# Forward transform: the stationary operand of two of eight pieces of x, 128 columns wide instead of twice 64

## The chip, the cores and the metric

One core of a Trainium2 chip runs the whole kernel in one launch. The metric is the device time of an execution in microseconds (us). TensorE is PE in the profile (its loads of stationary operands are PEld), VectorE is DVE, ScalarE is ACT, GpSimd is POOL, SyncE is SP.

## The reference, cut to what matters

Two layers follow each other on x of 16 images, 64 channels, 128 x 128 pixels, all in fp32. The change is in the first step of the first layer, the two-dimensional Hartley transform, of which only 20 x 20 modes are used:

```python
def dht_2d(x):
    return (fftn(x, axes=(2, 3)).real - fftn(flip(x, axis=(2, 3)), axes=(2, 3)).imag)
...
x_ht = dht_2d(x)                                               # 16 x 64 x 128 x 128
out_ht[:, :, :20, :20] = compl_mul2d(x_ht[:, :, :20, :20], w1) # mixes channels per mode
y = gaussian_smoothing_4d(dht_2d(out_ht) / (H * W)) * mask
# second layer: group norm, AFNO on 32 x 32 modes, group norm, 1x1 features,
# two shared experts and 4 of 16 experts per image with GELU, residual
```

The transform is separable: a sum over the rows of an image with cosines and sines, then a sum over its columns. The kernel does both sums as matrix products, and folds the first layer's inverse, its smoothing and the second layer's group norm and spectrum into tables over modes.

## The kernel before, in words

The kernel has stages that follow each other. The forward transform takes x from DRAM and leaves 400 modes of each image and channel in x2. Then the modes are mixed (L294 to L365), then the spectrum goes through AFNO's two layers (from L420 on), and last, over most of the time, come the inverse transform, the features and the experts, image by image, in an order written out in PIECES (L965).

The forward transform loops over the 16 images (L263) and, in each, over eight pieces of eight channels (c0, L266). For a piece:

- SP loads xt, 128 rows x 8 channels x 128 columns, 512 KB (L268). Pool f_x has 10 such buffers, so that SP runs up to ten pieces ahead and then waits until PE has done with the oldest.
- PE multiplies each channel with fwd1, 128 x 64, of which 40 columns are cosines and sines of 20 frequencies (L273). The image is the stationary operand: 128 rows are summed over, and its columns become partitions of the result in PSUM, ps (pool f_p1, 4 buffers). The 128 columns go as two operands of 64: one matmul in each half of the array and of the partitions, written as `h` in L271 and L272.
- ACT copies ps to t1, turned so that the channels lie next to each other (L276).

When t1 has all 64 channels, `along_columns` (L225) is the second sum for that image: 40 matmuls (L233) with t1 as stationary operand, 128 x 64, and fwd2 as moving operand, into ps2. It is a generator: the loop runs it in portions behind pieces 1 to 5 of the next image (L279), so that the last image's portions come after the loop (L285). After its matmuls ACT copies half of ps2 (L238), DVE adds and subtracts to xm (L242 to L245) and adds xm, with the weights of the smoothing along the batch, to up to nine images of x2 (L254). When an image of x2 is complete, ACT writes its second half (L259, L260). ACT has one order: these two wait for DVE, and the copies of the next pieces (L276) stand behind them.

fwd2 is loaded on SP's queue after the first image's pieces (L281), the weights wk after all of x (L284). The loads of wn (L294) use memory that is free only when DVE has ended the transform.

The order on each engine in this stage is the program's, as the scheduler of the tile framework lets it stand.

Of the kernel before, what the change touches and what calls it, by code (L numbers as in the profile page):

```python
# [18 lines left out]
NB, C, N = 16, 64, 128  # L19
# [11 lines left out]
EC = 65  # L31
TILES = (0, 1, 2, 3, 6, 7, 4, 5)
EDGED = {0: (0, 16), 1: (64, 16), 4: (128, 16), 5: (192, 16), 2: (256, 1)}
BY_ACT = (0, 2, 4, 6)
CL = C // 2
NSL = 8
# [21 lines left out]
def constant_tables():  # L58
# [29 lines left out]
    for j in range(2):  # L88
# [3 lines left out]
        for r in (0, 64):  # L92
            inv2[r:r + 32, j], inv2[r + 32:r + 64, j] = np.cos(a32)[:, ns], -np.sin(a32)[:, ns]
    e_cols = np.concatenate([s_[8 * t:8 * t + 8] for t, (_, m) in EDGED.items() if m > 1 for s_ in sides] + [[32]])
    d1 = e1 - g1 * e
# [85 lines left out]
def hartley_afno_moe_kernel(ctx: ExitStack, tc: tile.TileContext, a: dict, out: bass.AP):  # L181
# [6 lines left out]
    def load(pool, name, shape, eng=None):  # L188
        t = pool.tile(shape, F32, name=name + "_sb", tag=name)
        src = a[name]  # L190
        if len(shape) == 3 and len(src.shape) == 2:
            src = src.rearrange("p (a b) -> p a b", b=shape[2])
        (eng or nc.sync).dma_start(t, src)
        return t
# [15 lines left out]
    with tc.tile_pool(name="modes", bufs=1) as mp:  # L210
# [6 lines left out]
        with tc.tile_pool(name="f_x", bufs=10) as xp, tc.tile_pool(name="f_t", bufs=2) as tp, \  # L217
                tc.tile_pool(name="f_c", bufs=1) as fc, \
                tc.tile_pool(name="f_p1", bufs=4, space=PSUM) as pp1, \
                tc.tile_pool(name="f_p2", bufs=2, space=PSUM) as pp2:  # L220
            fwd1 = load(fc, "fwd1", [P, W1], nc.gpsimd)
            fwd2 = None
            seen = set()

            def along_columns(b, t1):  # L225


                ps = pp2.tile([P, K // 2, W1], F32, name="ps2")
                for m in range(K // 2):
                    for t in range(2):  # L230
                        for h in range(2):
                            j = 2 * (2 * m + h) + t
                            nc.tensor.matmul(ps[h * C:(h + 1) * C, m, :], lhsT=t1[:, j, :],  # L233
                                             rhs=fwd2[:, j, :], start=(t == 0), stop=(t == 1))
                    if m in (1, 3, 5, 7):
                        yield
                pn = tp.tile([P, K // 2, K], F32, name="pn")
                nc.scalar.copy(pn, ps[:, :, K:2 * K])  # L238
                xm = tp.tile([P, K, K], F32, name="xm")
                for half, op in ((0, ALU.add), (1, ALU.subtract)):  # L240
                    to = xm[half * C:(half + 1) * C]
                    nc.vector.tensor_tensor(to[:, 0:1], ps[0:C, 0:1, 0:K], pn[0:C, 0:1], op)  # L242
                    nc.vector.tensor_tensor(to[:, 2:K:2], ps[0:C, 1:, 0:K],
                                            pn[0:C, K // 2 - 1:0:-1], op)
                    nc.vector.tensor_tensor(to[:, 1:K:2], ps[C:P, :, 0:K],  # L245
                                            pn[C:P, ::-1], op)
                xf = xm.rearrange("p a b -> p (a b)")
                for bo in range(NB):
                    g = float(gb[bo, b])
                    if g == 0.0:  # L250
                        continue
                    to = x2[:, 0, bo, :]
                    if bo in seen:
                        nc.vector.scalar_tensor_tensor(to, xf, g, to, ALU.mult, ALU.add)  # L254
                    else:
                        nc.vector.tensor_scalar(to, xf, g, None, ALU.mult)
                        seen.add(bo)
                    if not gb[bo, b + 1:].any():
                        nc.scalar.mul(x2[0:C, 1, bo], x2[C:P, 0, bo], -1.0)  # L259
                        nc.scalar.copy(x2[C:P, 1, bo], x2[0:C, 0, bo])  # L260

            behind = None
            for b in range(NB):  # L263

                t1 = tp.tile([P, 2 * K, C], F32, name="t1")
                for c0 in range(0, C, 8):  # L266
                    xt = xp.tile([P, 8, N], F32, name="xt")
                    nc.sync.dma_start(xt, a["x"][b, :, c0:c0 + 8])  # L268
                    ps = pp1.tile([P, 8, W1], F32, name="ps1")
                    for i in range(8):  # L270
                        for h in range(2):  # L271
                            cols = slice(h * 64, (h + 1) * 64)  # L272
                            nc.tensor.matmul(ps[cols, i, :], lhsT=xt[:, i, cols],  # L273
                                             rhs=fwd1, start=True, stop=True)
                    src = ps[:, :, 0:2 * K].rearrange("p c j -> p j c")
                    nc.scalar.copy(t1[:, :, c0:c0 + 8], src)  # L276

                    if c0 and behind:
                        next(behind, None)  # L279
                behind = along_columns(b, t1)  # L280
                fwd2 = fwd2 or load(fc, "fwd2", [P, 2 * K, W1])  # L281

            for k in range(K // 2 + 1):
                nc.sync.dma_start(wk[0:C, k], a["w"][k])  # L284
            for _ in behind:  # L285
                pass

        with tc.tile_pool(name="m_o", bufs=1) as op, tc.tile_pool(name="m_w", bufs=4) as wp, \
# [24 lines left out]
            for h in range(2):  # L313
                hs_ = slice(h * CL, (h + 1) * CL)
                for ri in range(2):
                    own_rows = slice(h * C + ri * CL, h * C + (ri + 1) * CL)
                    for ro in range(2):
                        c0 = (ri ^ ro) * P + h * CL
# [99 lines left out]
    with tc.tile_pool(name="s_o", bufs=1) as so, \  # L418
# [86 lines left out]
        for r in range(4):  # L505
            g = slice(r * CL, (r + 1) * CL)
            c0 = (r & 1) * C + (r >> 1) * CL
# [121 lines left out]
        for b in range(NB):  # L629
            xk = sw.tile([P, MD * MD], F32, name="xk")  # L630
            xr = sw.tile([P, MD * MD], F32, name="xr")
            for n in range(2):
                cols = slice(n * 512, (n + 1) * 512)
# [31 lines left out]
    with s3:  # L665
# [59 lines left out]
        def pixels(box, t):  # L725
# [13 lines left out]
            def evacuate():  # L739
# [3 lines left out]
                pv = ps.rearrange("p s (j i) -> p i (s j)", i=C)  # L743
                e0, nm = EDGED.get(t, (0, 0))
                at = 4 if nm > 1 and t not in BY_ACT else 0
                if t in BY_ACT:
                    nc.scalar.copy(hv, pv)
# [311 lines left out]
```

## Time and profile before

| | us |
|---|---|
| median of 3 runs | 1706.57 (1701.43 to 1714.94) |
| profiled execution, its own time | 1737.26 |
| its span, first to last instruction | 1735.3 |
| L273, first to last start | 6.3 to 239.0 |
| PE, DVE, ACT busy in the span | 1561.7, 1268.7, 1272.2 |
| PE busy from 90 to 140 us | 38.46 of 50 |
| last load of x issued | 211.8 |

A row of a group reads: line, engine, operation, output<-inputs, stationary operand (rows*columns), moving operand (rows x columns), count, then busy time in us, mean duration in ns, and the idle time of the engine just before, with what ended it. An fp32 matmul of the program stands there as two loads (LDWEIGHTS) and two matmuls (MATMUL). Matmuls are pipelined: one is shown as longer than the time until the next starts, so starts are compared here. "issue" is idle time that ended with nothing the profile shows. A row of stretches has its length, then busy time and count of PE, PEld, DVE, ACT and POOL, the granted clock of PE as a share, the busy share of the DMA engines, and GB/s. Queue rows give packets, MB and the share of 16 DMA engines.

### The profile page before, as it was taken

To read this page: it belongs to the slowest core of one execution; us is meant where nothing else is said; L and a number is where in the kernel's file an instruction comes from. 1 tells how busy PE (TensorE), PEld (TensorE's weight loads), DVE (VectorE), ACT (ScalarE), POOL (GpSimd) and SP (SyncE) were. 2 spreads that over 40 slices of the span, in tenths; PEclk is the share of its full clock that TensorE was granted. 3 is DMA by queue.
4 is the path that set the end of the run, shared out by engine and by line. 5 is a ranking of instruction groups with operands and counts; after the bars stand their busy time and mean duration, and the time that the engine had idled before them with its cause. 6 is when DMAs were issued, how large, how long until landed. Compare 5 with 4: busy or idle time off the path is not lost.

```text
span 1735.3 us, 62072 instructions
## 1 busy us (share of the span) xinstructions
PE 1561.7 (90%) x27656; PEld 856.4 (49%) x27656; DVE 1268.7 (73%) x1700; ACT 1272.2 (73%) x1631; POOL 148.9 (9%) x152
## 2 busy tenths in 40 slices
PE   6778758799997999999999999999999999999974
PEld 6778755233325554454454455545555455544421
DVE  0344423365763698988989889898898988989886
ACT  2233334255664898988989889898898988989875
POOL 0000002000130101101010010100101001010020
PEclk9999979899996999999999999999999999999997
DMA  9888864353574224555545555455554554545447
GB/s 382 296 304 303 313 132 120 81 123 94 126 180 101 42 44 79 92 87 88 74 80 87 92 89 75 77 86 94 87 73 78 90 93 87 73 80 79 66 66 114
DMA packets 398864, 205.07 MB, mean 118 GB/s; under 512 B 366842, under 2 KB 371942, under 8 KB 396222
## 3 DMA queue, kind: packets, MB, share of 16 engines
q1 hardware_dynamic: 394134, 193.76, 52.7%
q0 software_dynamic: 4464, 7.35, 1.7%
q8 instruction: 217, 3.56, 0.8%
q14 instruction: 49, 0.40, 0.1%
HBM read 109.86 MB, written 91.20 MB: 116 GB/s over the span
## 4 chain that ended last, share of the span: by engine, by line
PE 79%; issue 7%; DMA 4%; DVE 4%; ACT 3%; SPq 1%; POOL 0%; DVEq 0%; POOLq 0%; ACTq 0%
PE pe L897 37%; PE pe L736 9%; PE pe L716 7%; PE pe L807 6%; PE psx L639 6%; PE ps L273 6%; PE ps L233 3%; DMA spec_sb<-in_spec_dram 1%; PE psd L561 1%; ACT g L902 1%; PE psd L540 1%; DVE h L906 1%; PE pso L587 1%; PE pso L575 1%; DMA fwd_sb<-in_fwd_dram 1%
## 5 line engine op out<-in xcount | busy, mean ns | idle before, releaser
L902 ACT ACTIVATE g<-pe,wl 128x1024 f32<-128x1024 f32 x512 | 553.7, 1210 | 12.3 <-PE pe L897 12.2
L897 PE MATMUL pe<-f,wl 64*64 64x512 f32 x4096 | 501.3, 607 | 5.5 <-DMA wl<-exd,ati 5.5
L906 DVE SCALAR_TENSOR_TENSOR h<-g,wt,h 128x1024 f32<-128x1024 f32 x384 | 472.2, 1279 | 32.9 <-ACT g L902 32.0
L902 ACT ACTIVATE g<-pe,vec_sb 128x1024 f32<-128x1024 f32 x256 | 269.0, 1114 | 80.3 <-PE pe L897 80.2
L906 DVE SCALAR_TENSOR_TENSOR h<-g,h 128x1024 f32<-128x1024 f32 x256 | 301.9, 1216 | 18.2 <-ACT g L902 18.2
L897 PEld LDWEIGHTS pe<-f,wl 64*64 64x64 f32 x4096 | 164.8, 136 | 220.1 <-issue 118.5
L897 PE MATMUL pe<-f,shw 64*64 64x512 f32 x2048 | 257.2, 618 | 1.3 <-DVE sco L849 0.4
L736 PEld LDWEIGHTS pe<-inv_sb,u 64*64 64x64 f32 x8192 | 170.8, 141 | 111.2 <-issue 85.8
L736 PE MATMUL pe<-inv_sb,u 64*64 64x64 f32 x8192 | 181.7, 226 | 36.6 <-issue 35.3
L273 PE MATMUL ps<-fwd_sb,xt 128*64 128x64 f32 x4096 | 155.5, 232 | 41.3 <-issue 35.0
L273 PEld LDWEIGHTS ps<-fwd_sb,xt 128*64 128x64 f32 x4096 | 144.7, 146 | 47.7 <-issue 41.4
L276 ACT COPY t<-ps 128x320 f32<-128x320 f32 x128 | 53.9, 426 | 150.9 <-PE ps L273 150.4
L912 DVE SCALAR_TENSOR_TENSOR stg<-g,wt,h 128x1024 f32<-128x1024 f32 x128 | 158.3, 1278 | 0.0
L811 ACT ACTIVATE f<-pe,fba 128x1024 f32<-128x1024 f32 x128 | 154.6, 1219 | 3.0 <-PE pe L807 2.9
L716 PEld LDWEIGHTS pe<-inv_sb,bm 116*64 116x64 f32 x4096 | 129.1, 142 | 52.7 <-ACT g L902 34.9
L716 PE MATMUL pe<-inv_sb,bm 116*64 116x64 f32 x4096 | 138.0, 228 | 2.1 <-issue 1.3
L807 PE MATMUL pe<-h,fsa 64*64 64x512 f32 x1024 | 133.4, 594 | 1.4 <-DVE h L751 1.4
L639 PE MATMUL psx<-spec_sb,ot 100*32 100x512 f32 x1024 | 118.7, 606 | 10.5 <-DMA spec_sb<-in_spec_dram 10.5
L242 DVE TENSOR_TENSOR xm<-ps,pn 64x20 f32<-64x20 f32 x32 | 5.5, 171 | 162.9 <-ACT pn L238 162.7
L897 PEld LDWEIGHTS pe<-f,shw 64*64 64x64 f32 x2048 | 73.8, 136 | 101.4 <-issue 71.1
L870 POOL TENSOR_TENSOR dv<-root_e,dv 128x4 f32<-128x4 f32 x16 | 34.6, 2164 | 1020.3 <-DVE ati L873 907.5
L749 DVE COPY h<-pe 128x960 f32<-128x960 f32 x64 | 75.9, 1185 | 58.9 <-PE pe L736 58.9
(186 smaller groups left out, 1244.8 us busy)
## 6 DMA issues: line engine op xcount, KB each, us to landing
xt<-in_x_dram SPq DMA_DIRECT2D x128, 512.0 KB
out_dram<-stg SPq DMA_DIRECT2D x217, 256.0 KB
bmd<-bs SPq DMA_DIRECT2D x32, 512.0 KB
bm<-bmd SPq DMA_DIRECT2D x64, 256.0 KB
out_dram<-stg SPq DMA_DIRECT2D x31, 192.0 KB
wk<-in_w_dram SPq DMA_DIRECT2D x11, 320.0 KB
wn<-in_w_dram SPq DMA_DIRECT2D x11, 320.0 KB
spec_sb<-in_spec_dram SPq DMA_DIRECT2D x1, 3200.0 KB
```

The costliest lines, as they stand in the source:

```text
L273: nc.tensor.matmul(ps[cols, i, :], lhsT=xt[:, i, cols], rhs=fwd1, start=True, stop=True)
L276: nc.scalar.copy(t1[:, :, c0:c0 + 8], src)
L639: nc.tensor.matmul(ps[p0:p0 + CL], lhsT=ot[:, kc, b * C + h * CL:b * C + (h + 1) * CL], rhs=spec[:, kc, ri * 1024 + n * 512:ri * 1024 + (n ...
L716: nc.tensor.matmul(ps[s * C:(s + 1) * C, i // 8, i % 8], lhsT=bm[0:KR, 16 * q + i], rhs=inv1[0:KR, s], start=True, stop=True)
L736: nc.tensor.matmul(ps[half * C:(half + 1) * C, s, j * C:(j + 1) * C], lhsT=u[rs, t * 8 + j], rhs=inv2[rs, half], start=True, stop=True)
L749: nc.vector.tensor_copy(hv[:, at:], pv[:, at:])
L807: nc.tensor.matmul(ps[p * C:(p + 1) * C, half], lhsT=fsa[rows_, box["b"]], rhs=box["h"][t][rows_, p], start=True, stop=True)
L811: nc.scalar.activation(f, ps, AF.Gelu, bias=fba[:, box["b"]:box["b"] + 1], accum_out=box["sums"][:, t:t + 1])
L897: nc.tensor.matmul(ps[half * C:(half + 1) * C, p], lhsT=w[rows_], rhs=f[rows_, half], start=True, stop=True)
L902: newest[0] = nc.scalar.activation(g, ps, AF.Gelu, bias=bias)
L906: nc.vector.scalar_tensor_tensor(h, g, share(), h, ALU.mult, ALU.add)
L912: nc.vector.scalar_tensor_tensor(box["out"][-1][:, :, c0:c0 + 16], gv, share(), hv, ALU.mult, ALU.add)
```

## The change

In pieces 2 and 6 of each image (c0 of 16 and 48) each channel is one matmul with all 128 columns as stationary operand and one result over all 128 partitions. The other six pieces stay as they are. The loads of x, the tables, the buffers and the copies are the same.

```diff
+AS_WHOLE = (2, 6)
+WHOLE, SIDES = (slice(0, N),), (slice(0, N // 2), slice(N // 2, N))
...
                     for i in range(8):
-                        for h in range(2):
-                            cols = slice(h * 64, (h + 1) * 64)
+                        for cols in (WHOLE if c0 // 8 in AS_WHOLE else SIDES):
                             nc.tensor.matmul(ps[cols, i, :], lhsT=xt[:, i, cols],
                                              rhs=fwd1, start=True, stop=True)
```

## The prediction

> **What bounds the kernel now.** I read the page first. Over the span TensorE (PE) looks like the bound, and the instruction queue moves next to nothing:
>
> ```profile
> PE 1561.7 (90%) x27656; PEld 856.4 (49%) x27656; DVE 1268.7 (73%) x1700; ACT 1272.2 (73%) x1631; POOL 148.9 (9%) x152
> ...
> q8 instruction: 217, 3.56, 0.8%
> ...
> L273 PE MATMUL ps<-fwd_sb,xt 128*64 128x64 f32 x4096 | 155.5, 232 | 41.3 <-issue 35.0
> ```
>
> The changed line, L273, runs only from 6.3 to 239.0 us, so what counts is what bounds that stretch. In the waits of PE, from 5 to 242 us, and in those of SP's queue, the reader is to see who is late:
>
> ```profile
> PE ps L273 <- issue: 35.0, 21, 3.6
> PE ps L233 <- issue: 11.5, 9, 2.2
> PE ps L233 <- ACT t L276: 9.4, 7, 1.9
> ```
>
> ```profile
> SPq L268 <- PE ps L273: 138.9, 109, 4.3
> ```
>
> PE never waits for a tile of x; SP waits 109 times for PE to give an xt buffer back. So x is early and PE sets the pace. But PE itself stands still 30 times, 46.5 us, for "issue": nothing that the view can name. The timeline, matmul rows only, shows the pattern (start, duration, count, and in brackets the idle time before it):
>
> ```profile
> 99.80 0.27 PE L233 MATMUL ps<-fwd_sb,t 128*64 128x64 f32 x2 [1.60 <-issue]
> ...
> 104.99 2.02 PE L273 MATMUL ps<-fwd_sb,xt 128*64 128x64 f32 x62 [1.23 <-issue]
> ...
> 110.21 0.97 PE L273 MATMUL ps<-fwd_sb,xt 128*64 128x64 f32 x26 [0.95 <-issue]
> ...
> 110.97 0.69 PE L233 MATMUL ps<-fwd_sb,t 128*64 128x64 f32 x16
> ...
> 111.44 1.15 PE L273 MATMUL ps<-fwd_sb,xt 128*64 128x64 f32 x32
> ...
> 112.37 0.57 PE L233 MATMUL ps<-fwd_sb,t 128*64 128x64 f32 x12
> ...
> 112.72 1.15 PE L273 MATMUL ps<-fwd_sb,xt 128*64 128x64 f32 x32
> ...
> 113.65 0.51 PE L233 MATMUL ps<-fwd_sb,t 128*64 128x64 f32 x9
> ...
> 114.83 0.33 PE L233 MATMUL ps<-fwd_sb,t 128*64 128x64 f32 x3 [0.67 <-issue]
> ...
> 120.50 0.74 PE L273 MATMUL ps<-fwd_sb,xt 128*64 128x64 f32 x18 [1.70 <-issue]
> ```
>
> From the stall at 110.21 to that at 114.83 there are 26+16+32+12+32+9 = 127 matmuls, each with one load: about 256 instructions. Queue 8 moved 217 packets and PE ran 55,312 instructions: 255 per packet, and 3.56 MB over 217 is 16.4 KB. So I read "issue" as PE waiting for its next 256 instructions. Ends of stalls lie 5.19, 5.22, 4.62 and 5.67 us apart, 5.2 us a block, while 128 matmuls at 29 ns (32 in the 0.93 us from 101.23 to 102.16) need 3.7 us. A block comes back later than it is used up.
>
> [...] Two such loads in a row stand at L824:
>
> ```profile
> 571.32 0.64 PE L716 MATMUL pe<-inv_sb,bm 116*64 116x64 f32 x16
> ...
> 571.88 0.30 PEld L824 LDWEIGHTS pe<-gs,g1w_sb 128*128 128x128 f32 x2
> ...
> 301.61 3.60 PE L452 MATMUL psx<-ot,dev_sb 100*100 100x512 f32 x8
> ```
>
> One load lasts 188 ns and both 0.30 us, so they follow at 0.11 us[...]. [...] L716's last matmul lasts 0.22 us and ends at 571.96, so it began at 571.74, and L824 begins 0.14 us later where pairs follow at 0.058.
>
> **The change part by part.**
>
> 1. Instructions. Each fp32 matmul stands as two matmuls and two loads in the trace (4096 of L273 for 16x8x8x2 calls). A piece has 32 matmuls; whole, 16. With 32 pieces changed, 512 matmuls and 512 loads go: 1024 instructions, exactly 4 blocks of 256, so later blocks keep their borders. L273 and L233 together go from 42 blocks to 38. At 5.2 us a block this alone, if the fetch still sets the pace, is -21 us.
>
> 2. PE's own time. Two 64-column matmuls in the two halves of the array start together, a pair each 58 ns: a piece takes 16 x 58 = 0.93 us. Whole, a load of 128 columns every 108 ns; the matmul beside it is shorter (L452 gives (3.60-0.59)/7 = 0.43 us for 512 columns, so 54 ns for 64) and I let it lie beside the next load, as it does now. That is 16 x 0.108 = 1.73 us, plus about 0.09 for the drain going in and 0.12 coming out (L824 to L897 shows the same 0.07 us before the modelled end; 64 columns make the last matmul 0.05 longer than L824's). So 1.94 us, 1.0 more than now, 32 times: +32 us. PE's work in the stage goes from 42 x 3.7 = 156 to 188 us, or from 3.7 to 4.95 us a block. Not shown is a load of 128 columns beside matmuls of 64. Its ends are 0.93 us (no dearer than the pair) and 16 x (108+54) + 0.2 = 2.8 us (load and matmul one after the other). I take 1.94.
>
> 3. Stalls. Blocks take 1.24 us more, so a stall for instructions shrinks by as much. The chain of waits lists the stalls; those over 1.24 are 2.31, 2.24, 2.44, 1.56, 1.61, 1.53, 1.86, 1.60, 1.70, 1.67, 2.21, 2.08, 1.75, 1.66, 1.69, 2.58 and 3.58, and what is over sums to 13 us, 12 for 38 blocks. So 46.5 falls to 12: -34 us. This is the cover of part 2; without it, its 32 us would be paid.
>
> 4. ACT's wait. L233's first group of an image waits 7 times, 9.4 us, for t's last columns, because ACT stands behind DVE at L260 before it copies. Piece 6 runs in that time, and hides up to 0.9 us of each wait: between 0 and -6.6, I take -5. What is late next there is the same copy.
>
> 5. x and the fetch share the DMA engines. A block now covers 3.05 pieces (84 instructions each), then 3.37 (76): from 1.60 MB in 5.2 us, about 305 GB/s, to some 325. When x was loading at full rate, blocks came slower:
>
> ```profile
> 8.00:40.00 32.00, 23.82 (x701) 23.13 (x698) 3.06 (x11) 8.31 (x20) 0.00 (x0) 0.95 1.02 410
> ...
> 90.00:140.00 50.00, 38.46 (x1234) 37.23 (x1229) 23.11 (x59) 17.78 (x41) 0.00 (x0) 1.00 0.90 313
> ```
>
> There the stalls end 6.3 us apart (22.18, 28.44, 34.84, 41.03). A straight line from 5.2 at 313 to 6.3 at 410 adds 0.2 us at 20 GB/s more; I take half, on the 20 or so blocks that still stall: +2.5, ends 0 and +8.
>
> 6. Clock. Stalls of over 2 us are followed by spells at half clock (PEclk 0.93 from 140 to 190, 0.77 from 212 to 242). Fewer long stalls, fewer spells: -3, ends -6[...].
>
> SP's order, ACT's copies, PSUM buffers and DVE are untouched; the same ps1 tile is written. What follows (wn's loads wait for DVE at 248.4, then spec's) moves as a whole with the end of the stage.
>
> Sum: +32 - 34 - 5 + 2.5 - 3 = -7.5 us. The profiled execution, 1737.26 us for a span of 1735.3, would come to about 1730. It lies 1.8% above the median of the runs, 1706.57; I take the same -7 off that: 1699.5.
>
> **The rivals.** *The fetch stays the only bound* (0.28): blocks come back at 5.2 us whatever PE does, the 32 us all fit in stalls, ACT waits and half-clock spells: -21 us, about 1686. For it: three of four blocks stall now. Against it: 4.95 us a block is close to 5.2, and returns scatter (4.6 to 6.3), so the quick ones are wasted. *PE becomes the bound* (0.20), the slower side: in whole pieces the load does not lie beside the matmul, 2.8 us a piece. PE's work rises by 60, stalls fall by some 41, ACT's wait by 7, half-clock spells add 6: +18 us, about 1725. It decides where a whole piece takes more than some 2.2 us, where the sum changes sign. For it: no row shows such loads and matmuls in a row at full width. Against it: L452's loads of 100 columns lie wholly beside its matmuls. *Nothing is gained* (0.10): x, let go faster, holds the fetches up by as much as is saved (part 5 at its upper end): within 3 us of before.
>
> **How the numbers follow.** My forecast, most of the gain traded for PE time, has 0.42: -16 to +2 us by its own terms, 1691 to 1709. About 1%, 17 us, is what a measurement of this kernel can tell from no change. Faster by over 1%: most of the first rival and a tail of the forecast, 0.36; slower: most of the second, 0.19; within: 0.45. The range takes in -26 (all of part 1, 4 and 6) to +18: 1680 to 1725.
>
> **What would show it.** In the changed profile: L273 with 3584 matmuls, 512 of them 128 wide, starting 108 ns apart; q8 with 213 packets; "issue" before L273 and L233 down from 46.5 to 10 to 20 us; L233's wait for ACT about halved; the last L273 some 7 us before 239. A spacing of 160 ns shows the second rival, stalls as long as now the last one. Wrong altogether would be stalls no longer 256 instructions apart.

## The result, and the profile after

Over 18 runs of each the changed kernel took 1695.02 us (median; 1689.81 to 1705.51), the kernel before 1703.84 (1696.10 to 1717.33). The ratio is 0.9954, 95% interval 0.9935 to 0.9973: some 8 us faster (4.6 to 11 by the interval), where 7 were forecast. The profiled execution of the changed kernel took 1696.35 us by itself.

The page of the changed kernel has the counts that the change promises:

```profile
span 1693.5 us, 61048 instructions
...
PE 1559.1 (92%) x27144; PEld 846.6 (50%) x27144; DVE 1268.4 (75%) x1700; ACT 1273.8 (75%) x1631; POOL 153.3 (9%) x152
...
q8 instruction: 213, 3.49, 0.8%
```

That is 512 matmuls, 512 loads and four packets of instructions fewer: 1024 instructions for four packets, 256 each. (Lines from 33 on have moved by one or two: L273 is L274, L233 is L235, L276 is L277, L268 is L270, L254 is L256.) The groups of PE up to 245 us, kept apart by shape, say which matmuls are whole and what stood idle before them:

```profile
L274 PE MATMUL ps<-fwd_sb,xt 128*64 128x64 f32 x3072 | 112.0, 226 | 13.6 <-issue 7.6 <-DMA fwd_sb<-in_fwd_dram 5.9
...
L274 PE MATMUL ps<-fwd_sb,xt 128*128 128x64 f32 x512 | 64.8, 279 | 1.2 <-issue 1.2
```

PE's waits in the stage, in the columns total us, times, longest:

```profile
PE ps L274 <- issue: 8.8, 9, 4.0
...
PE ps L235 <- issue: 4.4, 5, 2.2
PE ps L235 <- ACT t L277: 3.6, 9, 0.5
```

Against 35.0 + 11.5 us of "issue" and 9.4 us of ACT before, 13.2 and 3.6 are left. Two stretches of the middle of the stage, with the columns as in the prediction:

```profile
90.00:140.00 50.00, 47.26 (x1152) 45.52 (x1151) 21.11 (x56) 17.63 (x42) 0.00 (x0) 1.00 0.91 318
140.00:190.00 50.00, 47.25 (x1144) 45.48 (x1144) 21.13 (x57) 16.61 (x41) 0.00 (x0) 1.00 0.93 321
```

PE counts as busy for 47 of 50 us where it was 38.5 in the first of these stretches: it is close to the bound now. The chain of waits shows a whole piece, the portion of L235 behind it and a split piece in a row, and later the step that follows the stage:

```profile
128.76 1.93 PE ps L274 x16
130.69 0.73 PE ps L235 x20
131.43 0.93 PE ps L274 x32
...
235.56 4.08 DMA wn<-in_w_dram
```

The timeline of the changed kernel has the 16 loads of that whole piece within 1.86 us (128.69 to 130.55), one of them 0.19 us long, so they follow at 0.11 us; from the start of its last matmul to that of L235's next (130.42 to 130.62) 0.20 us pass. The prediction and two expectations call such pauses at a change of shape drains; what PE does in them is not shown.

wn's first load on that chain started at 248.42 before, so the stage ends 12.9 us earlier between these two single executions; the medians differ by 8.8. Their spans differ by 41.8 us, and that is not the change: from DVE's last addition of the stage (248.4 before, 235.5 after) to the end it is 1487 us in the one and 1458 in the other. The same stretch took 1452 to 1462 us in all four experiments on one chip, 1479 to 1481 in the four on a second and 1483 to 1491 in the four on a third, whatever was done to the stage. It seems to go with the chip (the chip of the first two is not on record). So below, ratios come from runs beside the kernel before on the same chip, and traces are compared only within the stage.

### The profile page after: what moved, and what is told of

Its sections match the earlier page's. It is cut to its first block, busy times and chain, and to the rows that moved or that the text cites. A ratio compares the mean times of both kernels' runs of the same rounds, so it can differ in the third digit from the quotient of the medians.

```text
span 1693.5 us, 61048 instructions
## 1 busy us (share of the span) xinstructions
PE 1559.1 (92%) x27144; PEld 846.6 (50%) x27144; DVE 1268.4 (75%) x1700; ACT 1273.8 (75%) x1631; POOL 153.3 (9%) x152
## 4 chain that ended last, share of the span: by engine, by line
PE 70%; DMA 9%; issue 9%; ACT 5%; DVE 4%; SPq 1%; POOL 1%; DVEq 0%; POOLq 0%; ACTq 0%
PE pe L898 31%; PE pe L717 7%; PE ps L274 7%; PE psx L640 6%; PE pe L737 6%; PE pe L808 5%; DMA wl<-exd,ati 5%; ACT g L903 3%; PE ps L235 3%; DMA spec_sb<-in_spec_dram 1%; PE psd L562 1%; PE psd L541 1%; DVE h L907 1%; PE pso L588 1%; DMA edge_sb<-in_edge_dram 1%
## 5 line engine op out<-in xcount | busy, mean ns | idle before, releaser
L898 PE MATMUL pe<-f,wl 64*64 64x512 f32 x4096 | 496.3, 606 | 40.5 <-DMA wl<-exd,ati 39.3
L898 PEld LDWEIGHTS pe<-f,wl 64*64 64x64 f32 x4096 | 148.2, 135 | 267.2 <-issue 153.5
L903 ACT ACTIVATE g<-pe,vec_sb 128x1024 f32<-128x1024 f32 x256 | 269.2, 1115 | 10.9 <-PE pe L898 10.8
L898 PE MATMUL pe<-f,shw 64*64 64x512 f32 x2048 | 244.2, 595 | 0.8 <-DVE sco L850 0.4
L274 PE MATMUL ps<-fwd_sb,xt 128*64 128x64 f32 (+1 forms) x3584 | 175.4, 234 | 14.8 <-issue 8.8
L737 PEld LDWEIGHTS pe<-inv_sb,u 64*64 64x64 f32 x8192 | 154.6, 141 | 67.5 <-issue 41.3
L274 PEld LDWEIGHTS ps<-fwd_sb,xt 128*64 128x64 f32 (+1 forms) x3584 | 162.8, 148 | 19.4 <-issue 10.0
L277 ACT COPY t<-ps 128x320 f32<-128x320 f32 x128 | 53.8, 427 | 151.3 <-PE ps L274 150.9
L737 PE MATMUL pe<-inv_sb,u 64*64 64x64 f32 x8192 | 157.6, 226 | 2.4 <-issue 1.3
```

Source lines behind the costliest of these rows:

```text
L274: nc.tensor.matmul(ps[cols, i, :], lhsT=xt[:, i, cols], rhs=fwd1, start=True, stop=True)
L737: nc.tensor.matmul(ps[half * C:(half + 1) * C, s, j * C:(j + 1) * C], lhsT=u[rs, t * 8 + j], rhs=inv2[rs, half], start=True, stop=True)
L898: nc.tensor.matmul(ps[half * C:(half + 1) * C, p], lhsT=w[rows_], rhs=f[rows_, half], start=True, stop=True)
L903: newest[0] = nc.scalar.activation(g, ps, AF.Gelu, bias=bias)
```

## The experiments

All twelve, with the changed kernel first; "chip" is the median of the kernel before beside it. "Issue" and "ACT" are PE's waits in the stage (us, one profiled execution each). "Half" is the length of the spells at half clock (granted clock 0.50) that begin between 8 and 215 us, by the trace's clock record; where it is empty, no sum was made. "End" is DVE's last addition. Ratios with their intervals are formed over all runs, so they can differ a little from the quotient of two medians.

Two things limit what these columns say. The profiled executions of only_6, only_2, six_seven, x_on_15 and one_five took 6.6 to 12.9 us more than the median of their kernel, so their stalls and spells are not the usual size. And the clock record begins only with the first change to full clock: at 8.9 to 15.2 us in the kernels with an entry under "half", but at 28.8 us in three_whole and at 38.5 us in all_whole. Ahead of that PE went at half pace, as the first image's pieces of these two show (208 and 128 matmuls):

```profile
6.14 20.22 PE L274 MATMUL ps<-fwd_sb,xt 128*64 128x64 f32 x208 [6.14 <-DMA fwd_sb<-in_fwd_dram]
```

```profile
6.20 27.57 PE L274 MATMUL ps<-fwd_sb,xt 128*128 128x64 f32 x128 [6.20 <-DMA fwd_sb<-in_fwd_dram]
```

The first row is five split and three whole pieces (its shape is that of the first matmul). At 0.93 and 1.93 us they would take 10.4 us; the eight whole pieces of the second would take 15.4. Neither the column "half" nor a run's mean clock counts this time.

| kernel | chip | median | ratio (95%) | issue | ACT | half | end |
|---|---|---|---|---|---|---|---|
| before, profiled | | 1706.57 | | 46.5 | 9.4 | 13.7 | 248.4 |
| after (2, 6) | 1703.84 | 1695.02 | 0.9954 (0.9935-0.9973) | 13.2 | 3.6 | 3.4 | 235.5 |
| x_once_split | 1704.65 | 1641.30 | 0.9623 (0.9587-0.9659) | 7.1 | 0.5 | | 183.7 |
| x_once_whole | 1704.65 | 1674.52 | 0.9815 (0.9776-0.9853) | 1.5 | 1.0 | | 215.4 |
| only_6 | 1704.65 | 1699.85 | 0.9966 (0.9930-1.0003) | 33.3 | 2.0 | 23.9 | 248.1 |
| all_whole | 1704.65 | 2019.21 | 1.15 to 1.19, single runs | 0 | 8.2 | | 548.5 |
| only_2 | 1732.99 | 1732.90 | 0.9996 (0.9979-1.0013) | 25.2 | 11.3 | 41.0 | 253.6 |
| three_whole | 1732.99 | 1735.84 | 1.0018 (1.0007-1.0028) | 4.1 | 6.3 | 0 | 249.5 |
| six_seven | 1732.99 | 1742.79 | 1.0054 (1.0037-1.0070) | 27.3 | 4.6 | 34.1 | 260.3 |
| x_on_15 | 1732.99 | 1792.95 | 1.0331 (1.0296-1.0366) | 21.9 | 10.2 | | 307.9 |
| two_six_beside | 1728.48 | 1721.76 | 0.9952 (0.9933-0.9971) | 16.6 | 3.7 | 0 | 238.2 |
| one_five | 1728.48 | 1728.36 | 1.0015 (0.9997-1.0033) | 9.1 | 14.0 | 37.5 | 259.3 |
| x_four | 1728.48 | 1732.21 | 1.0022 (1.0010-1.0034) | 29.7 | 5.2 | 3.4 | 246.9 |
| three_seven | 1728.98 | 1729.42 | 0.9999 (0.9980-1.0019) | 21.2 | 5.1 | 3.4 | 244.0 |

### Is it the loads of x that make instructions late?

Both kernels load only the first ten pieces of x and use these buffers in turn; x_once_split multiplies as before, x_once_whole as the changed kernel.

```diff
-        with tc.tile_pool(name="f_x", bufs=10) as xp, tc.tile_pool(name="f_t", bufs=2) as tp, \
+        with tc.tile_pool(name="f_x", bufs=1) as xp, tc.tile_pool(name="f_t", bufs=2) as tp, \
...
-            behind = None
+            behind, kept = None, []
...
-                    xt = xp.tile([P, 8, N], F32, name="xt")
-                    nc.sync.dma_start(xt, a["x"][b, :, c0:c0 + 8])
+                    piece = b * 8 + c0 // 8
+                    if piece < 10:
+                        kept.append(xp.tile([P, 8, N], F32, name=f"xt{piece}"))
+                        nc.sync.dma_start(kept[piece], a["x"][b, :, c0:c0 + 8])
+                    xt = kept[piece % 10]
```

> The kernel before, but only the first ten pieces of x are loaded, and their ten buffers are used again and again: 118 of 128 loads of x are left out. If PE's stalls are blocks of instructions that wait behind x on the DMA engines, then without x a block is back before the 3.7 us in which it is used up: waits of L273 and L233 for issue fall from 46.5 us to under 10 after the start, and the stage comes to its 156 us of matmuls plus ACT's waits and the start, so that L273 ends near 190 us rather than 239: about 45 us faster than before. If a block takes 5.2 us to come whatever x does, or if the stalls are something else than instructions, they stay, and the time moves by less than 10 us.

> The same, but with pieces 2 and 6 whole as in the changed kernel; 118 of 128 loads of x are left out here too. If the change trades PE time for stalls, there is nothing left to trade: the 32 whole pieces cost their 1.0 us more each, less what fits into ACT's waits, and this kernel is 20 to 30 us slower than the same without whole pieces. If the fetch keeps its pace of 5.2 us a block without x, it is still some 8 us faster than that one.

The stretch from 90 to 140 us of x_once_split:

```profile
90.00:140.00 50.00, 50.00 (x1721) 50.00 (x1719) 30.16 (x79) 23.95 (x57) 0.00 (x0) 1.00 0.02 5
```

and of x_once_whole:

```profile
90.00:140.00 50.00, 50.00 (x1246) 48.85 (x1247) 23.47 (x61) 19.23 (x45) 0.00 (x0) 1.00 0.01 3
```

With 3 to 5 GB/s in place of 313, PE is busy 50 of 50 us: 1721 matmuls at 29 ns. PE's instructions are the same as before in number and order (27656 matmuls, 217 packets on q8), so it was the loads of x that made them late. The 63 us gained are more than the 45 expected: ACT's wait went with the stalls (9.4 to 0.5), and from 38 to 184 us there is no spell at half clock.

Between these two kernels the change costs: 1674.52 - 1641.30 = 33.2 us (four runs of each, which spread over 6 and 10 us), or 1.04 us for each of the 32 whole pieces; 20 to 30 had been expected. This is close to the prediction's second part (+32 us, 1.0 a piece). It is a net figure: stalls for issue also go from 7.1 to 1.5 us. The same edit that gains 8 us beside the loads of x loses 33 without them: it gains only where its extra time falls into waits, of the fetch and of ACT.

### How many pieces?

Each kernel differs from the changed one in one line:

```diff
-AS_WHOLE = (2, 6)
+AS_WHOLE = (6,)                # only_6
+AS_WHOLE = (2,)                # only_2
+AS_WHOLE = (2, 4, 6)           # three_whole
+AS_WHOLE = tuple(range(8))     # all_whole
```

> Only piece 6 whole, the one that runs while ACT stands behind DVE. By the trade: +16 us of PE time, 40 blocks of 4.3 us instead of 42 of 3.7, stalls from 46.5 to some 27, ACT's waits from 9.4 to some 4.5: about 7 us faster than before, nearly all of what both pieces bring. If every whole piece brought the same, half of the change: 4.4 us.

> Only piece 2 whole. The trade gives +16 us of PE time and stalls down from 46.5 to some 27, as with piece 6 alone, but ACT's waits of 9.4 us stay: about 3 us faster than before. If piece 6 hid nothing more than this one, both single pieces bring the same.

> Pieces 2, 4 and 6 whole. By the trade 36 blocks of 5.7 us: only the longest stalls are left, some 3 us, so the third piece pays its 16 us of PE time nearly in full and takes away only some 9 us of stalls: between 6 us faster than before and 3 slower, so slower than the change with two. A rival is the clock: all_whole ran at half clock from 55 us on; if three whole pieces of eight are enough for that, the stage doubles and the kernel is 100 us or more slower.

> All eight pieces whole. If PE time replaces stalls: 26 blocks of instructions instead of 42, no stalls left, but an image takes 8 x 1.73 us for its pieces, 2.3 for L233 and some 1.3 for the drains between the two, 17.4 us, so that the stage ends near 285 us: 40 to 50 us slower than before. If a whole operand were better by itself, it would gain four times the change's 8.8 us.

PE's waits of only_6, then of only_2, up to 250 us:

```profile
PE ps L274 <- issue: 23.9, 16, 3.4
PE ps L235 <- issue: 9.4, 5, 4.4
...
PE ps L235 <- ACT t L277: 2.0, 6, 0.5
```

```profile
PE ps L274 <- issue: 22.2, 17, 4.2
PE ps L235 <- ACT t L277: 11.3, 11, 1.5
...
PE ps L235 <- issue: 3.0, 4, 1.1
```

Piece 6 removes the wait for ACT (9.4 to 2.0), piece 2 does not (11.3). Either alone leaves 25 to 33 us of stalls. only_6 gained 4.8 us where 7 were expected, and its interval holds both the change's 0.9954 and no change; only_2 gained nothing where 3 us were expected. Its trace, of its slowest run, has 41.0 us at half clock.

Three whole pieces remove most of the stalls, and the kernel is no faster (2.9 us slower by the medians, 6 faster to 3 slower expected). Waits, then a stretch, of three_whole:

```profile
PE ps L235 <- ACT t L277: 6.3, 12, 0.5
...
PE ps L274 <- issue: 4.1, 2, 2.8
```

```profile
40.00:90.00 50.00, 50.00 (x1085) 48.31 (x1083) 14.59 (x39) 13.45 (x33) 0.00 (x0) 1.00 0.92 323
```

PE is busy 50 of 50 us at full clock here, and 47.9 and 48.4 in the two stretches of 50 us that follow: it is the bound, and the 16 whole pieces more, at 1.04 us each, find few stalls to lie in. But that is not the whole loss. The stage ends 11.3 us later than that of two_six_beside (on another chip), and the first image is 8 us of it (20.22 us for its pieces in place of 12.19), because full clock came at 28.8 us and not at 10.8; only 1 of these 8 us is the third whole piece. Whether it comes so late in every run of three_whole is not on record. So of one, two and three pieces two had the lowest ratio, but only_6 cannot be told from it, and a third piece might be nearly as good with a start like the others'.

all_whole missed its expectation of 40 to 50 us more: the fastest of its four runs took 259 us more, the others 308 to 321, among them the profiled one. The stretches of its trace, and one piece from its timeline:

```profile
8.00:40.00 32.00, 31.48 (x195) 31.11 (x196) 0.00 (x0) 3.65 (x9) 0.00 (x0) 1.00 0.72 266
60.00:500.00 440.00, 433.82 (x2644) 415.12 (x2643) 71.86 (x186) 57.75 (x134) 0.00 (x0) 0.50 0.41 121
```

```profile
102.93 3.68 PE L274 MATMUL ps<-fwd_sb,xt 128*128 128x64 f32 x16
```

The 1.00 of the first stretch is only the lack of a record until 38.5 us; its first eight pieces took 3.45 us each. The record then has 17.1 us at full clock and 488.1 at half. From 60 to 500 us PE counts as busy for 434 of 440 us, and the clock stayed at 0.50: a piece takes 3.68 us in place of 1.93. In all some 520 us were at half clock. At full clock they would have been 260, and the stage would have ended near 288 us (an estimate): the expectation had 285, so what it had wrong is the clock. Two of the runs list a mean clock of 0.973 and still took 2026 us; a record that begins only after the stage would give that, but their traces were not kept. The clock records show two levels, 1.00 and 0.50, and in the stage spells at 0.50 of 3.4, 6.8 and 10.2 us beside these 488.1. What sets the level is not shown. It is not the profile's busy share alone: 434 of 440 us went with 0.50 here, and 50 of 50 with 1.00 in x_once_split, x_once_whole and three_whole. A piece of whole operands is 16 loads at 0.11 us (as measured in the changed kernel at full clock) with a matmul of some 54 ns beside each (the prediction's estimate from L452), and a PE that did little else in the stage was granted half the clock.

### Which pieces?

> Pieces 6 and 7 whole, next to each other: one pair of drains less an image (3 us in all), and both in the time in which ACT stands behind DVE, so that its 9.4 us of waits go. But a block with two whole pieces takes 6 us and needs no cover, while the blocks without one keep their stalls, some 20 us: about 6 us faster than before, like the change. If 3.9 us of whole operands in a row make the clock fall to half, slower than before.

> The changed kernel once more, beside the two that follow on the same chip. If the gain is the change's and not one chip's: ratio 0.993 to 0.997, stalls for issue in the forward stage some 10 to 20 us where before has 40 to 50, the wait for ACT 3 to 5. The rival, that part of the 8.8 us was the order of the clock's spells on one chip: within 0.2% of before.

> Pieces 1 and 5 whole in place of 2 and 6: the same distance of four, the same number of instructions and of matmuls. If all that counts is how evenly PE's extra time lies among the blocks of instructions, it equals the changed kernel within 0.2%. If piece 6 matters because it covers the wait for ACT at the first group of L233 (9.4 us before), that wait stays at 8 to 11 us and this kernel is 3 to 6 us slower than the changed one. The rival, that the wait for ACT is covered by any whole piece: it falls to 3 to 5 us here as well.

> Pieces 3 and 7 whole. In an image ACT copies piece 5 to t1 before it copies ps2's half (pn), on which DVE and then ACT's next copies wait, so that a whole piece 5 lengthens the chain that the next image's first group of L233 waits for, and a whole piece 6 or 7 lies beside it. If that is why pieces 1 and 5 gained nothing, 3 and 7 do as 2 and 6 do: the wait for ACT 3 to 6 us, ratio 0.993 to 0.998, few spells at half clock. The rival, that 2 and 6 are two lucky places among the blocks of instructions: the wait for ACT may be small too, but the time is within 0.2% of before.

```diff
-AS_WHOLE = (2, 6)
+AS_WHOLE = (6, 7)    # six_seven
+AS_WHOLE = (1, 5)    # one_five
+AS_WHOLE = (3, 7)    # three_seven
```

Two neighbours are the worst of the four (1.0054). Their timeline, PE alone:

```profile
131.16 0.39 PE L235 MATMUL ps<-fwd_sb,t 128*64 128x64 f32 x6 [2.26 <-issue]
131.49 6.87 PE L274 MATMUL ps<-fwd_sb,xt 128*128 128x64 f32 x32
```

A stall of 2.26 us, then the clock falls at 131.8 for 10.2 us (0.50 in the stretch from 132 to 142), and both whole pieces are done at that clock: 6.87 us in place of 3.9. In before and x_four all five spells that begin between 8 and 215 us are 3.4 us long; in the kernels of the table with whole pieces and an entry under "half" 14 of 22 are 6.8 or 10.2. Whole pieces are not the only way to long spells: x_on_15, which has none, has three of 6.8 us, x_once_split one of 6.8 and one of 10.2. Over its 19 runs six_seven has a mean clock of 0.9509 beside 0.9556 for before: 0.0047 of 1733 us is 8.1 us, so by the record at most that much of the 9.8 that it lost is clock.

The changed kernel again, beside the next two: 0.9952, within 0.0002 of the first chip, with these waits:

```profile
PE ps L274 <- issue: 12.5, 12, 4.0
...
PE ps L235 <- issue: 4.1, 4, 1.6
PE ps L235 <- ACT t L277: 3.7, 9, 0.5
```

So the gain is the change's and not one chip's. Pieces 1 and 5, as far apart and as many, gained nothing: 6.6 us slower than the changed kernel by the medians (3 to 6 expected, if piece 6 matters for ACT's wait). The wait for ACT did not fall; at 14.0 it is above the 8 to 11 expected. The timeline of one_five shows why:

```profile
99.45 2.00 PE L274 MATMUL ps<-fwd_sb,xt 128*128 128x64 f32 x16
...
101.38 0.45 PE L235 MATMUL ps<-fwd_sb,t 128*64 128x64 f32 x8
...
101.88 0.33 ACT L240 COPY pn<-ps 128x200 f32<-128x200 f32 x1
...
103.89 3.49 DVE L256 SCALAR_TENSOR_TENSOR x<-xm,x 128x400 f32<-128x400 f32 x7
...
105.59 0.75 ACT L277 COPY t<-ps 128x320 f32<-128x320 f32 x2
...
106.07 0.68 PE L235 MATMUL ps<-fwd_sb,t 128*64 128x64 f32 x14 [1.44 <-ACT t L277]
```

The whole piece at 99.45 is piece 5, and the last eight matmuls of L235 stand behind it. From their end (101.83) it goes over ACT's pn, DVE and ACT to the copy that the next image's first group waits for, 4.2 us; PE has pieces 6, 7 and 0 meanwhile, 2.8 us. A whole piece 6 lies beside that chain and makes it 3.8; a whole piece 5 lies ahead of it and covers nothing.

That wait may have a second price. In the stretches after it:

```profile
107.50:114.10 6.60, 6.60 (x95) 6.48 (x95) 0.64 (x2) 0.85 (x2) 0.00 (x0) 0.50 0.64 214
114.30:124.30 10.00, 8.56 (x213) 8.22 (x210) 5.03 (x14) 3.81 (x9) 0.00 (x0) 1.00 0.82 276
124.60:131.20 6.60, 6.60 (x98) 6.48 (x99) 0.50 (x2) 0.85 (x2) 0.00 (x0) 0.50 0.66 216
```

A gap of 1.7 us between PE's starts in each image, a spell of 6.8 us some 1.4 us after its end, and the next image the same, 17.0 us later, four in a row. This execution took 1741.28 us, 12.9 above the kernel's median, so it shows this at its strongest and not the usual size. Each run of one_five lists its mean clock over the whole kernel, and the 22 go from 1723.5 us at 0.963 to 1746.5 at 0.950. A difference of 0.013 of 1735 us is 22.6 us of full clock; the times differ by 23.0. So time and clock go together from run to run here; that it is the gaps of this stage that make the slow runs slow is argued from one trace, not shown.

three_seven was to settle this, and did so by half. Its waits:

```profile
PE ps L274 <- issue: 13.8, 12, 3.0
...
PE ps L235 <- issue: 7.4, 3, 4.0
...
PE ps L235 <- ACT t L277: 5.1, 11, 0.5
```

A whole piece 7 covers the wait for ACT as piece 6 does (5.1). But the kernel is no faster than before (0.9999), against my theory's 0.993 to 0.998. The profile has 4.6 us more of stalls than two_six_beside and a stage that ends 5.8 us later, with 3.4 and 0 us of spells. The mean clocks of all runs on this chip, over the whole kernel, say what the clock can have to do with it:

| kernel | runs | mean us | mean clock | us against before if all of it counts (of 1720) |
|---|---|---|---|---|
| before | 64 | 1728.6 | 0.9567 | |
| two_six_beside | 8 | 1721.2 | 0.9595 | -4.8 |
| three_seven | 14 | 1728.6 | 0.9562 | +0.9 |
| one_five | 22 | 1731.8 | 0.9570 | -0.5 |

(2, 6) lies 7.4 us under both before and (3, 7), and at most 4.8 and 5.7 us of that are recorded clock. It may be less: over these 64 runs of before 0.001 of mean clock goes with 0.8 us and not 1.7, x_four has a higher mean clock than before (0.9580) and is slower, and the profiled executions of (2, 6) and (3, 7) have nearly the same clock (0.961 and 0.960) and part in their stalls. So why (2, 6) gains and (3, 7) does not stays open: the rival of that expectation, lucky places among the blocks of instructions, fits the time but was not tested by itself. For one_five the mean clock is that of before; what it saves in stalls it gives back in ACT's wait and in PE's own time.

### Can the loads be kept out of the way of the fetch?

x_on_15 loads each piece of x, in the kernel before, as 120 and 8 partitions, which was assumed to leave one of the 16 DMA engines without x; x_four gives the kernel before 4 buffers for x.

```diff
-                    nc.sync.dma_start(xt, a["x"][b, :, c0:c0 + 8])
+                    nc.sync.dma_start(xt[0:120], a["x"][b, 0:120, c0:c0 + 8])
+                    nc.sync.dma_start(xt[120:P], a["x"][b, 120:P, c0:c0 + 8])
```

```diff
-        with tc.tile_pool(name="f_x", bufs=10) as xp, tc.tile_pool(name="f_t", bufs=2) as tp, \
+        with tc.tile_pool(name="f_x", bufs=4) as xp, tc.tile_pool(name="f_t", bufs=2) as tp, \
```

> The kernel before, with each piece of x loaded as 120 partitions and 8 partitions, two DMAs[...]. If PE's instructions come over the last engine, they no longer wait behind x: stalls fall below 10 us[...]: 30 to 45 us faster. If they come over another engine, that one is busier than before, stalls stay or grow, and the time moves by less than 8 us or up.

> The kernel before with 4 buffers for x in place of 10, so that at most four loads of x are on the way or unread. If the fetch of instructions waits behind the loads of x that stand in the DMA queues before it, blocks come back sooner, the stalls for issue fall from about 46 to under 30 us, and PE waits for x instead in part: between 10 us faster and 10 us slower. If only the rate of x counts (over 300 GB/s in this stage with either number), the stalls for issue stay at 40 to 50 us and the time within 5 us. In the first 40 us, where ten loads were sent at once, the pace of blocks should come from 6.3 to nearer 5.3 us by the first, and stay by the second.

x_on_15, a stretch and the first of its waits:

```profile
90.00:140.00 50.00, 34.13 (x964) 31.88 (x960) 16.62 (x43) 12.80 (x30) 0.00 (x0) 0.97 0.93 245
```

```profile
PE ps L274 <- DMA xt<-in_x_dram: 39.1, 43, 2.5
```

The first theory had 30 to 45 us faster, the second less than 8 us of difference or slower; it is 60 us slower. x itself became slow (245 GB/s), and PE now waited for it. That one engine stayed without x was not shown: the views of the trace do not name engines, and the DMA busy share, 0.93 to 0.94 from 40 to 190 us, is 0.91 to 0.95 in the changed kernel too. Stalls for issue fell to 21.9, but in a stage that waits elsewhere this says nothing on which DMA engine carries the instructions, or whether they wait behind x on one; that stays open.

x_four, waits and the first stretch:

```profile
PE ps L273 <- issue: 21.3, 19, 2.3
PE ps L273 <- DMA xt<-in_x_dram: 15.4, 24, 2.0
PE ps L233 <- issue: 8.4, 8, 1.9
```

```profile
8.00:40.00 32.00, 23.35 (x652) 22.01 (x651) 3.06 (x11) 7.88 (x19) 0.00 (x0) 1.00 0.88 307
```

Stalls are 29.7 us in place of 46.5, as the first theory has it, and from 8 to 40 us only one of 0.8 where before has 5.9. But PE waits 15.4 us for x instead, nearly what the stalls lost, and part of the stalls may lie hidden in these waits: that instructions come sooner with fewer loads on the way is not shown, as in x_on_15. PE's 23.35 busy us in the first stretch are no more than before's 23.82, so the pace there did not rise to that theory's 5.3 us a block, and the whole is 0.2% slower. With four buffers for x one wait is traded for another, without gain.

None of the kernels that load all of x has a lower ratio than the changed one.

## Why the prediction was right, point by point

The forecast was a trade of -7.5 us; 8.8 and 6.7 were measured on two chips (differences of medians).

1. *Instructions.* Right: 512 matmuls and 512 loads, four packets less.
2. *PE's own time.* Right: a whole piece stands at 1.93 us in the chain of waits (1.94 forecast), and x_once_whole against x_once_split puts 1.04 us net on each (1.0). The length in the trace also ends the rival in which the load does not lie beside the matmul, at 2.8 us.
3. *Stalls.* Right in size: 13.2 and 16.6 us are left where 12 were forecast and 46.5 stood. The x_once pair shows that the edit gains nothing without waits to cover, of the fetch or of ACT.
4. *ACT's wait.* Right: 3.6 and 3.7 left for 4.4 forecast, and only_6, only_2, one_five and three_seven show that a whole piece does it that runs after L235's last group, 6 or 7, as the step says of piece 6.
5. *x and the fetch.* The rate rose to 318 and 321 GB/s (325 forecast). On the page of before q1, which x and other loads take, has 52.7% and q8, the instructions, 0.8% of the same 16 engines' span; which engines carry the one or the other is not shown. The +2.5 us for it was measured by no run; x_once_split shows only that instructions come in time when x is not loading at all.
6. *Clock.* The sign was right on record, the size is not settled: for -3 us the mean clocks give -4.8 at most, and the profiles of the changed kernel have 3.4 and 0 us of spells for 13.7. The step's reading was too strong: of the seven gaps of over 2 us between PE's starts from 8 to 215 us in before, four are followed by a spell. With the same sums for parts 1 to 3, (3, 7) and (1, 5) gained nothing; how much of that is clock is open. The step's sum had no loss of clock by whole pieces themselves; six_seven lost 9.8 us, by the record at most 8.1 of it clock. My expectation for all_whole failed by this term: it had 1 us a piece and no half clock.

The first rival (the fetch as the only bound, -21 us) falls with the interval of the ratio, which ends at 11 us, and with PE busy 47 of 50 us. The last one (nothing gained) is ruled out for (2, 6) on two chips. But that the sum came within 2 us is in part luck: terms of +32 and -34 leave a remainder that a few us of stalls or clock can erase, as (3, 7) shows, to which the same terms apply.

## What to carry to other kernels

When instructions come late, a form with fewer of them that takes longer costs little as long as its extra time falls into the stalls (here it gained 8.8 and 6.7 us beside the loads of x, and cost 33.2 without them); take no more of it than fills them (with eight whole pieces, at half clock, the kernel was 259 us slower or more), and try it with the cause of the stalls taken away to see its bare price. Of several places for the longer work, one beside a chain that ends in a wait hid that wait here (9.4 us before, 2.0 in only_6, 5.1 in three_seven), and one ahead of the chain did not (14.0 in one_five). Where a gain is the small remainder of two large terms, look at the clock of every run, and at where its record begins, before a place is called better.

## What had not been expected of the hardware

- Half clock often follows short gaps. Between 8 and 215 us, before's four spells each follow a gap of 2.2 to 2.5 us between PE's starts, beginning 3.2 to 3.6 us ahead of the fall. The chain of waits and a stretch of before:

```profile
139.22 2.21 issue
```

```profile
142.40:145.40 3.00, 3.00 (x62) 3.00 (x62) 0.00 (x0) 0.62 (x2) 0.00 (x0) 0.50 0.62 201
```

  Of all 27 spells there in the kernels of the table with a "half" entry, 24 begin within 4 us of the start of a gap of 1.4 to 2.8 us; not every such gap is followed by one (4 of 24 over 1.2 us in before). Five gaps of 1.7 us in one_five were each followed by a spell.
- A PE that mostly loads whole operands for 64-column matmuls kept half clock for 488 us while the profile shows it 98% busy (all_whole). That whole pieces draw a spell out is suggested by six_seven's 10.2 us, not shown.
- The clock record says nothing until the first change to full clock, 8.9 to 38.5 us from the start here, while PE goes at about half pace where the first image shows it (20.22 us for work of 10.4 in three_whole, 27.57 for 15.4 in all_whole); the mean of 1.00 that all_whole has from 8 to 40 us means no record up to 38.5.
- Some 30 of 42 blocks of 256 instructions cost up to 3.6 us each in this stage beside some 300 GB/s of loads (46.5 us in all), and next to nothing beside 5 GB/s: from 40 to 140 us of x_once_split PE is busy 99.96 of 100 us.
